# Layer 1's expert output bias: nine bf16 part pairs in one product of 96 rows instead of f32 products of 8 rows

## The chip, the cores and the metric

The kernel runs on one core of a Trainium2 chip. The core has five engines with queues of their own: TensorE (PE in the profile; its weight loads are shown apart as PEld), VectorE (DVE), ScalarE (ACT), GpSimd (POOL) and SyncE (SP), which here only issues transfers (DMAs). Each engine works through its queue in order; between engines there are semaphores. TensorE multiplies a stationary operand ("weights", loaded first) with a moving operand and writes to PSUM. The metric is the time of one execution in device microseconds (us), the median of the runs.

## The reference

Four layers act in turn on x of 625 rows (graph nodes) and 768 columns. Each layer is a graph step followed by a feed-forward step, both behind a layer norm and added to x. The feed-forward steps of layers 0, 1 and 3 are mixtures of eight experts with 192 hidden columns each; layer 1's also has attention in front, and it alone has a bias `b1` in the hidden columns and a bias `b2` of 8 x 768 at the output:

```python
        xn2 = _layernorm(x, norm2_w, norm2_b).reshape(-1, C)
        logits = xn2 @ w_gate
        top_vals, top_idx = jax.lax.top_k(logits, TOPK)
        gates = jax.nn.softmax(top_vals, axis=-1)
        gates_full = jnp.zeros((T, E), xn2.dtype).at[jnp.arange(T)[:, None], top_idx].add(gates)

        def body(acc, p):
            w1, bb1, w2, bb2, g = p
            h = jax.nn.gelu(xn2 @ w1 + bb1, approximate=False)
            return (acc + g[:, None] * (h @ w2 + bb2), None)
```

So each row of the output gets, besides the products, its eight gates times `b2`: a matrix product of 625 x 8 with 8 x 768.

## The kernel before

One program, written in program order; a scheduler orders each engine's queue by dependencies and expected times, so the queues are not always in the order of the source. The 625 rows lie in five tiles of P = 125 (`TILES`, NT = 5). All large products are in f32. One f32 product of a 128-row chunk shows in the profile as two records of L136 (in the helper `mm`) or as two matmul records of another line; a bf16 product as one.

**Experts** (`experts`, L962 and after), run for layers 0, 1 and 3:

1. `b1` and `b2` are loaded (L969 loads `b2` as `b2t`, 8 rows in f32), then the first weight matrix in three parts (L165 in `weight`; the pool of weights has four buffers, and later weights wait until an early one is free).
2. The first product makes `hg`, the 12 chunks of 128 hidden columns (8 experts x 192) for all rows, two chunks at a time, by a seven-product scheme in place of eight. `sums` (POOL, L338 to L342 in `half_products`) makes sums of weights, `first` begins a pair of chunks, `rest` ends it with PE products and DVE additions (L412) and ScalarE's gelu (L1001). `rest(c)` asks first for the sums of the next pair; the sums have two buffers, and POOL, which runs ahead, starts each when PE is through with the pair before last.
3. During the first `rest`, the router's logits (L250) are turned (L260), and `gates` (L917) computes on DVE the eight gates of each row in f32 (`lg`), and then, at L955 to L959, splits them into three bf16 parts `gb` whose sum is the f32 value: cast, subtract, cast, subtract, cast.
4. PE turns `gb` (L1025, five tiles) and DVE copies it to `gT3` (L1029): 24 rows (8 experts x 3 parts), 625 columns. In layer 1 PE also turns the f32 gates (L1033) and DVE copies them to `gT` (L1034): 8 rows.
5. `gate(c)` (L129, then L1009) spreads `gT3` with a 0/1 matrix `sel` over the chunk's 128 rows and multiplies `hg` with it, two pairs of chunks behind `rest`.
6. `down` (L1048): `hg` times the second weight matrix, quarters `q`. Tile 0 is done plainly: per half of 384 columns 12 chunks, and in layer 1 a 13th product of 8 rows, `gT` by `b2t`. Tiles 1 and 2, then 3 and 4, are done in pairs by seven products (`prod`, six chunks each); DVE makes sums of the weights (L444 to L447), POOL sums of `hg` (L464 to L468). The bias is appended to products 4, 2, 5 and 3. Product 3 enters one of the four output blocks alone, and what it adds there, together with product 5's bias of tile t + 1, has to be the bias of tile t; so it gets the difference of the gates of both tiles, `db`, made by POOL (L1094):

```python
                if b2t is not None and bias:
                    g, j = bias
                    lhs.append(db[:, t // 2] if g is None else gT[:, TILES[g]])
                    rhs.append(b2t[:, j * HD : (j + 1) * HD])
                self.mm(to, lhs, rhs)
```

The additions to x are DVE's (L1116), after a copy of the first product by ScalarE (`U`, L1124). When a tile is finished, `final` begins the next layer's norm (L178 to L191; the square root L182 is ScalarE's), and POOL adds the next layer's bias to x (L225).

**Beside layers 0 and 1's experts** runs other work of layer 3, `attention_vectors` (L1261): dot products on DVE (L1298, two for each block of weights `av_w`) with transfers of their own (L1278 `av_a`, L1287 `av_w`, two buffers). `beside(n, after)` puts n of them behind a given value (L1297 copies one element of it first).

**Around the start of layer 1's experts** SyncE's queue holds, in this order: three parts of the first weights, `b2t`, the first quarter of the second weights, `av_a` and `av_w`. On POOL stand there the sums of the first two pairs of chunks (L338 to L342), then L1525 (x plus the attention's output, last tile).

Of the kernel before, what the change touches and what calls it, by code (L numbers as in the profile page):

```python
# [9 lines left out]
F32 = mybir.dt.float32  # L10
BF16 = mybir.dt.bfloat16
# [6 lines left out]
N = 625  # L18
# [17 lines left out]
class Net:  # L36
# [880 lines left out]
    def gates(self, over_all):  # L917
# [35 lines left out]
        gb = sp.tile([P, NT, NEXP, 3], BF16, tag="gb", name="gb", bufs=1)  # L953
        r = sp.tile([P, NT, NEXP], F32, tag="gr", name="gr", bufs=1)
        nc.vector.tensor_copy(gb[:, :, :, 0], lg)  # L955
        nc.vector.tensor_tensor(r, lg, gb[:, :, :, 0], ALU.subtract)
        nc.vector.tensor_copy(gb[:, :, :, 1], r)
        nc.vector.tensor_tensor(r, r, gb[:, :, :, 1], ALU.subtract)
        nc.vector.tensor_copy(gb[:, :, :, 2], r)  # L959
        return gb  # L960

    def experts(self, over_all, w1, w2, gelu, b1=None, b2=None, after=None, beside=None):  # L962

        nc, tc, a, x = self.nc, self.tc, self.a, self.x
        with tc.tile_pool(name="moe", bufs=1) as big, ExitStack() as up_pool:
            bc = self.column(b1, NF) if b1 else None
            if b2:
                b2t = big.tile([NEXP, D], F32, name="b2t")
                nc.sync.dma_start(b2t, a[b2])  # L969
            hg = big.tile([128, NF, N], F32, name="hg")  # L970
            gT3 = big.tile([3 * NEXP, N], BF16, name="gT3")
            gT = big.tile([NEXP, N], F32, name="gT") if b2 else None
# [20 lines left out]
            def rest(c, between=None):  # L993
                if c + 2 < NF:
                    sums(c + 2)
                self.half_rest(
                    prods.pop(c), begun.pop(c), hg[:, c, :], hg[:, c + 1, :], between
                )
                for o in range(2):
                    h = self.n3(hg[:, c + o, :])  # L1000
                    nc.scalar.activation(  # L1001
                        h, h, gelu, bias=bc[:, c + o : c + o + 1] if b1 else 0.0
                    )

            def gate(c):
                gv = self.nv(self.ps(), 128)
                self.mm_nodes(gv, [sel[:, c * 128 : (c + 1) * 128]], [self.n3(gT3)])
                h = self.n3(hg[:, c, :])
                nc.vector.tensor_tensor(h, h, gv, ALU.mult)  # L1009
# [6 lines left out]
            turned, gb = self.logits(big), []  # L1016

            def choose():
                turned()
                gb.append(self.gates(over_all))  # L1020

            rest(0, choose)
            pv = self.nv(self.ps(), 3 * NEXP)
            for t in range(NT):
                nc.tensor.matmul(  # L1025
                    pv[:, t, :], gb[0][:, t].rearrange("p e i -> p (e i)"), self.identb[:P, :P],
                    start=True, stop=True,
                )
            nc.vector.tensor_copy(self.n3(gT3), pv)  # L1029
            if b2:  # L1030
                pv = self.nv(self.ps(), NEXP)
                for t in range(NT):
                    nc.tensor.transpose(pv[:, t, :], self.lg[:, t, :], self.ident[:P, :P])  # L1033
                nc.vector.tensor_copy(self.n3(gT), pv)  # L1034
            for c in range(2, NF + 2, 2):
                if c < NF:
                    if c not in begun:
                        first(c)
                    rest(c)
                for o in (c - 2, c - 1):  # L1040
                    gate(o)
                if beside and c < NF:
                    beside(1, hg[:P, c + 1, 0:1])
            up_pool.close()
            with tc.tile_pool(name="moedown", bufs=1) as dp:
                self.down(dp, a[w2], hg, gT, b2t if b2 else None, after, beside)

    def down(self, pool, w2, hg, gT, b2t, after, beside):  # L1048
# [14 lines left out]
        if b2t is not None:  # L1063
            db = pool.tile([NEXP, 2, P], F32, name="db")
# [7 lines left out]
        for j in range(2):  # L1072
            lhs = [hg[:, c, TILES[0]] for c in range(NF)]
            rhs = [q[c // HB][j][:, c % HB, :] for c in range(NF)]
            if b2t is not None:
                lhs.append(gT[:, TILES[0]])
                rhs.append(b2t[:, j * HD : (j + 1) * HD])
            self.mm(p[:, 512 * j : 512 * j + HD], lhs, rhs)
# [12 lines left out]
        def sums(t):  # L1091
            if b2t is not None:

                nc.gpsimd.tensor_tensor(  # L1094
                    db[:, t // 2], gT[:, TILES[t]], gT[:, TILES[t + 1]], ALU.subtract
                )
            prods[t] = list(zip(self.left_sums(pool, hg, t), rights))

        sums(1)
        for t in (1, 3):  # L1100
# [4 lines left out]
            def prod(n, to, bias=None):  # L1105
                A, B = pr[n - 1]
                lhs = [A[:, c, :] for c in range(HB)]
                rhs = [B[:, c, :] for c in range(HB)]
                if b2t is not None and bias:
                    g, j = bias  # L1110
                    lhs.append(db[:, t // 2] if g is None else gT[:, TILES[g]])
                    rhs.append(b2t[:, j * HD : (j + 1) * HD])
                self.mm(to, lhs, rhs)
# [17 lines left out]
            prod(4, b2, (t + 1, 0))  # L1131
# [10 lines left out]
            prod(2, a1, (t, 0))  # L1142
# [4 lines left out]
            prod(5, a2, (t + 1, 1))  # L1147
# [4 lines left out]
            prod(3, b1, (None, 1))  # L1152
# [1150 lines left out]
```

## Time and profile before

| what | value |
|---|---|
| three runs, median (lowest to highest) | 1932.52 us (1931.92 to 1932.81) |
| the profiled execution, its own time | 1933.47 us |
| its span, first to last instruction | 1931.8 us |
| PE busy, share of the span | 1855.9 us, 96% |
| DVE, ACT, POOL busy | 59%, 27%, 31% |
| mean granted clock of TensorE | 0.986 of full |
| DMA, mean | 53 GB/s |
| layer 0's, 1's and 3's turn of the gates (L1025) starts at | 258.97, 750.14, 1800.62 us |
| products with `b2t` in layer 1: records, first and last start | 20, from 816.2 to 892.2 us |

"Busy" counts the time in which an engine has an instruction in flight. TensorE's matmuls overlap each other and their ends are modelled, so the time between two starts says more than a record's length. "<-" behind a wait names what released it. A "stretch" is a piece of the span between two times.

### The profile page before, as it was taken

What the parts mean: (1) busy time and instruction counts of PE and PEld (TensorE: products, weight loads), DVE (VectorE), ACT (ScalarE), POOL (GpSimd) and SP (SyncE); (2) the same over time, 40 slices, a digit from 0 to 9 for tenths busy, and PEclk for the clock granted to TensorE, in tenths of its full rate; (3) what the DMA queues carried; (4) which work ended last, traced back from release to release, by engine and by line L of the source; (5) the groups of instructions that cost most, each with busy time, mean ns of one, the idle gap of its engine ahead of it and who ended that gap; (6) DMA issues with size and microseconds to landing.
All of it is one profiled execution on the core that took longest, in us unless ns stands there. A gap on an engine that the chain in (4) does not pass through costs nothing.

```text
span 1931.8 us, 21712 instructions
## 1 busy us (share of the span) xinstructions
PE 1855.9 (96%) x8314; PEld 1274.8 (66%) x8314; DVE 1134.9 (59%) x2226; ACT 526.2 (27%) x961; POOL 601.8 (31%) x515
## 2 busy tenths in 40 slices
PE   7968899999999999999999999999999999999999
PEld 6844565555677766655556778878667888556665
DVE  8789857647566756674835464554546555145562
ACT  2379611002254532100111131322314233111200
POOL 1079624234410052343015222231035321402331
PEclk9969899999999999999999999999999999999999
DMA  2040112120300022213510211000011121020111
GB/s 68 21 142 37 36 37 66 53 80 12 103 26 25 1 96 90 71 52 115 156 65 31 76 36 63 26 25 33 1 43 35 39 71 65 1 98 25 47 35 32
DMA packets 64021, 103.16 MB, mean 53 GB/s; under 512 B 7301, under 2 KB 37223, under 8 KB 63918
## 3 DMA queue, kind: packets, MB, share of 16 engines
q1 hardware_dynamic: 63658, 101.69, 16.2%
q8 instruction: 66, 1.08, 0.2%
q14 instruction: 37, 0.30, 0.1%
q10 hardware_dynamic: 260, 0.09, 0.0%
HBM read 99.81 MB, written 1.95 MB: 53 GB/s over the span
## 4 chain that ended last, share of the span: by engine, by line
PE 83%; DVE 7%; POOL 4%; ACT 2%; issue 1%; DMA 1%; SPq 1%; ACTq 0%; DVEq 0%; POOLq 0%
PE ps L136 65%; PE ps L129 3%; POOL gat_w L560 2%; PE ps L777 2%; PE ps L1806 2%; PE ps L1461 2%; PE ps L1493 2%; PE ps L1480 1%; PE ps L198 1%; PE ps L1675 1%; PE ps L143 1%; DMA av_w<-in_L_gnn_W 1%; PE ps L715 1%; DVE gat_w L591 1%; ACT gat_w L593 1%
## 5 line engine op out<-in xcount | busy, mean ns | idle before, releaser
L338 POOL TENSOR_TENSOR S<-w 128x384 f32<-128x384 f32 x40 | 41.5, 1042 | 453.6 <-PE ps L136 354.8
L136 PE MATMUL ps<-xT,w 128*128 128x313 f32 x480 | 137.9, 431 | 0.7 <-ACT pr L1469 0.7
L136 PE MATMUL ps<-w,xT 128*125 128x384 f32 (+2 forms) x392 | 125.3, 473 | 0.0
L136 PE MATMUL ps<-T,w 128*128 128x313 f32 x408 | 121.5, 428 | 0.0
L560 POOL TENSOR_TENSOR gat_w<-gat_w,xT 125x625 f32<-125x625 f32 x60 | 86.3, 1469 | 101.0 <-DVE xT L532 94.0
L136 PEld LDWEIGHTS ps<-xT,w 128*128 128x128 f32 x480 | 89.1, 190 | 35.1 <-issue 2.7
L136 PE MATMUL ps<-T,S 128*128 128x313 f32 x348 | 107.5, 444 | 1.8 <-DVE T L318 1.4
L136 PEld LDWEIGHTS ps<-w,xT 128*125 128x125 f32 x392 | 72.8, 188 | 46.6 <-issue 11.7
L136 PE MATMUL ps<-w,S 128*125 128x384 f32 x292 | 100.2, 488 | 2.8 <-DVE x L1116 2.8
L136 PE MATMUL ps<-xT,S 128*128 128x313 f32 x336 | 102.7, 433 | 0.0
L136 PE MATMUL ps<-w,hg 128*125 128x384 f32 x288 | 96.5, 488 | 0.9 <-DVE hg L1009 0.9
L136 PEld LDWEIGHTS ps<-T,w 128*128 128x128 f32 x408 | 76.0, 189 | 29.9 <-DVE U L358 1.4
L136 PE MATMUL ps<-hh,gat_w 125*125 125x257 f32 (+1 forms) x400 | 89.8, 379 | 0.0
L136 PEld LDWEIGHTS ps<-T,S 128*128 128x128 f32 x348 | 65.6, 195 | 30.7 <-issue 5.1
L136 PE MATMUL ps<-w,x2T 128*125 128x384 f32 (+1 forms) x280 | 84.1, 449 | 0.0
L136 PEld LDWEIGHTS ps<-w,S 128*125 128x125 f32 x292 | 54.3, 188 | 43.9 <-DVE x L1116 4.0
L136 PEld LDWEIGHTS ps<-hh,gat_w 125*125 125x125 f32 x400 | 73.3, 187 | 11.3 <-issue 0.4
L136 PEld LDWEIGHTS ps<-w,hg 128*125 128x125 f32 x288 | 53.1, 188 | 39.9 <-issue 2.2
L777 PE MATMUL ps<-ohd,ohs 125*125 125x313 bf16 x425 | 66.4, 312 | 12.2 <-DVE ohs L770 12.2
L136 PEld LDWEIGHTS ps<-xT,S 128*128 128x128 f32 x336 | 61.0, 189 | 25.0 <-issue 4.1
L1298 DVE CUSTOM_DVE_ANT_0 av_junk<-av_w,av_a 128x512 f32<-128x512 f32 (+1 forms) x80 | 72.2, 902 | 8.9 <-DMA av_w<-in_L_gnn_W 7.2
L569 DVE CUSTOM_DVE_ANT_0 junk<-ps,mb 125x625 f32<-125x625 f32 x85 | 68.5, 806 | 13.5 <-PE ps L143 8.7
(442 smaller groups left out, 3795.9 us busy)
## 6 DMA issues: line engine op xcount, KB each, us to landing
w<-in_L_ffn_phiT SPq DMA_DIRECT2D x8, 1536.0 KB
w<-in_L_gnn_W SPq DMA_DIRECT2D x8, 1536.0 KB
w<-in_L_ffn_w SPq DMA_DIRECT2D x6, 1152.0 KB
w<-in_L_gnn_W SPq DMA_DIRECT2D x6, 1152.0 KB
av_w<-in_L_gnn_W SPq DMA_DIRECT2D x24, 256.0 KB
av_w<-in_L_gnn_W SPq DMA_DIRECT2D x16, 384.0 KB
w<-in_L_ffn_w SPq DMA_DIRECT2D x3, 1536.0 KB
w<-in_L_ffn_qkv_wT SPq DMA_DIRECT2D x6, 768.0 KB
```

The source lines that it names most:

```text
L129: self.nc.tensor.matmul(pv[:, s, :], lhs[i], rhs[i][:, s, :], start=i == 0, stop=i == n - 1)
L136: self.nc.tensor.matmul(out, lhs[i], rhs[i], start=i == 0, stop=i == n - 1)
L143: self.nc.tensor.transpose(pv[:, t, :], col(t).to_broadcast([P, rows]), self.ident[:P, :P])
L198: nc.tensor.transpose(pv[:, k, :P], src[:, k * 128 : (k + 1) * 128], self.ident[:P, :P])
L338: nc.gpsimd.tensor_tensor(S1, A21, A22, ALU.add)
L560: nc.gpsimd.tensor_tensor(w[:, s, :], w[:, s, :], lc[:, s, :], ALU.add)
L569: nc.vector.tensor_tensor_reduce(self.n3(junk), row, self.n3(mb[:, t, :]), 1.0, -3e38, ALU.subtract, ALU.max, m[:, t : t + 1],)
L777: nc.tensor.matmul(acc[j // 2][:, j % 2, :], ohs[:, TILES[j]], ohd[:, 0:HN], start=c == cs[0], stop=c == cs[-1],)
L1298: nc.vector.tensor_tensor_reduce(junk, wt, row, 1.0, 0.0, ALU.mult, ALU.add, dst)
L1461: nc.tensor.matmul(sv[r][:, s, :], qk[half[r], 0, TILES[t]], self.n3(qk[half[r], 1, :])[:, s, :], start=True, stop=True,)
L1493: nc.tensor.matmul(ov[half[r]], v[:, s, h * DH : (h + 1) * DH], pT[r][:, s, :], start=s == 0, stop=s == NT - 1,)
L1806: nc.tensor.matmul(pv[:, j, :], zTs[t][:, k, :], w2[k // 3][:, k % 3, js], start=k == 0, stop=False,)
```

## The change

- `gates` no longer makes a tile of its own, but writes into a tile `gb` that `experts` makes: for each row of x, `copies` groups of `rows` columns. In layers 0 and 3 this is one group of 24, as before; in layer 1 three groups of 32 (24 used, the rest set to zero by POOL). The third part is written directly by the last subtraction, in all three layers. In layer 1 two copies bring the 24 columns to the other groups.
- `gT3` has 96 rows in layer 1: three groups of the 24 parts of the gates. The f32 turn and `gT` are gone; `gate` reads the first 24 rows.
- `b2` is loaded nine times, so that 96 rows hold it: row 32 j + 3 e + i is `b2` of expert e (i and j from 0 to 2); the rows between are zero (POOL). `bias_parts`, seven operations of POOL behind the `rest` of chunks 6 and 7, makes the bf16 tile `b2p`: in group j the j-th bf16 part of `b2`. One product of 96 rows thus sums all nine pairs of a gate part and a bias part. `b2n` is the right half of it with the sign changed.
- In `down` the bias products are `gT3` by `b2p`, in bf16. Product 3 has two of them, tile t by the right half of `b2p` and tile t + 1 by `b2n`, in place of one by `db`; POOL's `db` is gone.

```diff
         nc.vector.tensor_tensor(lg, lg, den.to_broadcast([P, NT, NEXP]), ALU.mult)
-        gb = sp.tile([P, NT, NEXP, 3], BF16, tag="gb", name="gb", bufs=1)
         r = sp.tile([P, NT, NEXP], F32, tag="gr", name="gr", bufs=1)
-        nc.vector.tensor_copy(gb[:, :, :, 0], lg)
-        nc.vector.tensor_tensor(r, lg, gb[:, :, :, 0], ALU.subtract)
-        nc.vector.tensor_copy(gb[:, :, :, 1], r)
-        nc.vector.tensor_tensor(r, r, gb[:, :, :, 1], ALU.subtract)
-        nc.vector.tensor_copy(gb[:, :, :, 2], r)
-        return gb
+        parts = gb[:, :, 0, 0 : 3 * NEXP].rearrange("p t (e i) -> p t e i", i=3)
+        nc.vector.tensor_copy(parts[:, :, :, 0], lg)
+        nc.vector.tensor_tensor(r, lg, parts[:, :, :, 0], ALU.subtract)
+        nc.vector.tensor_copy(parts[:, :, :, 1], r)
+        nc.vector.tensor_tensor(parts[:, :, :, 2], r, parts[:, :, :, 1], ALU.subtract)
+        for j in range(1, gb.shape[2]):
+            nc.vector.tensor_copy(gb[:, :, j, 0 : 3 * NEXP], gb[:, :, 0, 0 : 3 * NEXP])
...
+            copies, rows = (3, 32) if b2 else (1, 3 * NEXP)
             if b2:
-                b2t = big.tile([NEXP, D], F32, name="b2t")
-                nc.sync.dma_start(b2t, a[b2])
+
+                b2t = big.tile([96, D], F32, name="b2t")
+                b2p = big.tile([96, D], BF16, name="b2p")
+                b2n = big.tile([96, D // 2], BF16, name="b2n")
+                nc.gpsimd.memset(b2t, 0.0)
+                for j in range(3):
+                    for i in range(3):
+                        r = 32 * j + i
+                        nc.sync.dma_start(b2t[r : r + 3 * NEXP - 2 : 3, :], a[b2])
             hg = big.tile([128, NF, N], F32, name="hg")
-            gT3 = big.tile([3 * NEXP, N], BF16, name="gT3")
-            gT = big.tile([NEXP, N], F32, name="gT") if b2 else None
+            gT3 = big.tile([copies * rows, N], BF16, name="gT3")
+            gb = big.tile([P, NT, copies, rows], BF16, name="gb")
+            if b2:
+                nc.gpsimd.memset(gb, 0.0)
...
+            def bias_parts(after):
+
+                nc.gpsimd.tensor_copy(b2p[:, 0:1], after)
+                nc.gpsimd.tensor_copy(b2p, b2t)
+                nc.gpsimd.tensor_tensor(b2t, b2t, b2p, ALU.subtract)
+                for j in range(1, 3):
+                    nc.gpsimd.tensor_copy(b2p[32 * j : 32 * j + 32, :], b2t[32 * j : 32 * j + 32, :])
+                nc.gpsimd.tensor_tensor(b2p[64:96, :], b2t[64:96, :], b2p[64:96, :], ALU.subtract)
+                nc.gpsimd.tensor_scalar(b2n, b2p[:, D // 2 :], -1.0, None, ALU.mult)
...
-            pv = self.nv(self.ps(), 3 * NEXP)
+            pv = self.nv(self.ps(), copies * rows)
...
             nc.vector.tensor_copy(self.n3(gT3), pv)
-            if b2:
-                pv = self.nv(self.ps(), NEXP)
-                for t in range(NT):
-                    nc.tensor.transpose(pv[:, t, :], self.lg[:, t, :], self.ident[:P, :P])
-                nc.vector.tensor_copy(self.n3(gT), pv)
...
                     rest(c)
+                    if b2 and c == 6:
+                        bias_parts(hg[:96, 5, 0:1])
...
-            if b2t is not None:
+            if bias:
                 lhs.append(gT[:, TILES[0]])
-                rhs.append(b2t[:, j * HD : (j + 1) * HD])
+                rhs.append(bias[0][:, j * HD : (j + 1) * HD])
...
-            if b2t is not None:
-
-                nc.gpsimd.tensor_tensor(
-                    db[:, t // 2], gT[:, TILES[t]], gT[:, TILES[t + 1]], ALU.subtract
-                )
...
+            bl, br, bn = bias[0][:, 0:HD], bias[0][:, HD:], bias[1]
...
-            prod(4, b2, (t + 1, 0))
+            prod(4, b2, (t + 1, bl))
...
-            prod(2, a1, (t, 0))
+            prod(2, a1, (t, bl))
...
-            prod(5, a2, (t + 1, 1))
+            prod(5, a2, (t + 1, br))
...
-            prod(3, b1, (None, 1))
+            prod(3, b1, (t, br), (t + 1, bn))
```

In the order of instructions of the changed kernel, which is fixed before it runs, nothing moves on ScalarE. On SyncE the first quarter of the second weights now stands ahead of the loads of `b2`. On DVE, in layer 1's first pair of tiles, the addition of product 2 to x (L1116) stands one dot product (L1298) earlier than before, and the additions of products 5 and 3 keep their place or stand up to one dot product earlier.

## The prediction

> **What bounds the kernel now.** I read first the share of the chain that ended last, by engine; then the list of what TensorE waits for; then the timeline of the three places where layer 1's bias and the gates are made; then the table of busy time by stretch with the granted clock; last, the comparison of the two kernels' instruction order, which needs no run.
>
> ```profile
> PE 83%; DVE 7%; POOL 4%; ACT 2%; issue 1%; DMA 1%; SPq 1%; ACTq 0%; DVEq 0%; POOLq 0%
> ```
> TensorE (PE) carries 83% of the chain: an instruction taken from PE is time, except where PE soon waits for something else. Those waits, in the list of waits of PE (total us, times, longest):
> ```profile
> PE ps L1025 <- DVE gb L959: 7.8, 3, 2.6
> ...
> PE ps L136 <- DVE x L1116: 2.8, 2, 1.6
> ```
> The change touches both. The first is the turn of the gates, once in each expert layer (0, 1, 3): PE has nothing to do for 2.6 us until VectorE (DVE) has split the gates in three bf16 parts. Layer 0, timeline (start, us, engine, line):
> ```profile
> 256.92 0.99 POOL L341 TENSOR_TENSOR w<-w 128x384 f32<-128x384 f32 x1
> 257.05 0.92 DVE L958 TENSOR_TENSOR gr<-gr,gb 125x40 f32<-125x40 f32 x1
> 257.87 0.99 POOL L342 TENSOR_TENSOR S<-w,S 128x384 f32<-128x384 f32 x1
> 258.00 0.92 DVE L959 CAST gb<-gr 125x40 bf16<-125x40 f32 x1
> 258.82 0.47 DVE L412 TENSOR_TENSOR hg<-hg,ps 128x313 f32<-128x313 f32 x1
> 258.97 0.27 PEld L1025 LDWEIGHTS <-gb 125*24 125x24 bf16 x5 [3.11 <-DVE gb L959]
> 258.97 0.45 PE L1025 MATMUL ps<-identb,gb 125*24 125x125 bf16 x5 [2.61 <-DVE gb L959]
> ```
> A DVE operation on 40 elements should be short: the cast of L955, before GpSimd (POOL) starts, takes 0.21. Those at L956 to L959 take 0.6 to 1.0, and each ends just after a POOL operation of L338 to L342 ends. While POOL works, each such step costs one POOL operation, whatever its size. And the wait has an after-effect (stretch; span of it and busy us of PE, PEld, DVE, ACT, POOL with counts; PEclk is the granted clock):
> ```profile
> 256.10:259.51 3.41, 0.80 (x7) 0.43 (x7) 3.17 (x5) 0.19 (x1) 2.76 (x3) 1.00 0.00 0
> 259.51:262.93 3.42, 3.42 (x7) 2.23 (x8) 0.92 (x2) 0.53 (x1) 0.00 (x0) 0.50 0.00 0
> 747.62:751.03 3.41, 0.89 (x10) 0.70 (x11) 3.17 (x5) 0.54 (x1) 2.41 (x3) 1.00 0.00 0
> 751.03:754.45 3.42, 3.42 (x9) 2.31 (x8) 1.12 (x3) 0.27 (x1) 0.00 (x0) 0.50 0.00 0
> ...
> 1798.92:1802.34 3.42, 1.72 (x10) 1.32 (x11) 2.78 (x4) 0.72 (x1) 1.59 (x2) 1.00 0.02 5
> 1802.34:1805.75 3.41, 3.41 (x14) 2.28 (x13) 0.71 (x2) 0.00 (x0) 0.00 (x0) 1.00 0.00 0
> ```
> A stretch of 3.41 us with PE busy 0.80 or 0.89 (23%, 26%) is followed by one at half clock, in layers 0 and 1. In layer 3 the same wait straddles two stretches, the emptier one is 50% busy, and the clock stays.
>
> **The change, part by part.** The sum is made against the profiled execution, 1933.47 us (span 1931.8 and 1.7 around it); the median of the runs, 1932.52, is 0.95 lower.
>
> (a) *Gates of layers 0 and 3.* One of the four DVE steps in POOL's shadow goes: the last subtraction writes bf16 itself. L958 ended at 257.97, L959 at 258.92: 0.95 us earlier for PE, twice: 1.9. From there the chain is PE, and the weight loads and POOL sums behind it are released by PE, so the gain travels on.
>
> (b) *The clock in layer 0.* With a wait of 2.61 - 0.95 = 1.66 us no stretch of 3.41 can be less than 51% busy, wherever it begins; 50% kept the clock in layer 3. So 259.51 to 262.93 should run at full clock: 3.42 / 2 = 1.7. Bounds 0 and 1.7; I take 1.7. [...]
>
> (c) *Gates of layer 1.* Here DVE has one step more: five become six (two copies of 24 bf16 columns added, one cast gone). The four POOL operations there end at 750.02 and L959 at 750.09; the first copy takes its place, the second follows when POOL is done: 0.2, the duration of L955 (0.95 if it had to wait for POOL again). Five f32 transposes of the gates (L1033, 750.51 to 751.05) go: -0.54. The turn now has 96 columns of weights, not 24: 0 to 0.13, as a 128-column load (L198) takes 0.13 and five follow each other. Sum -0.2, bounds -0.35 and +0.55. The wait stays near 2.7 us, so I leave layer 1's half clock where it is. L1034's copy (0.79 on DVE) goes too, before a DVE wait of 2.3 on PE: nothing.
>
> (d) *The price of a bias product.* PE rows, of layer 1's first output tile and of a gate product (24 rows, bf16) between f32 products:
> ```profile
> 816.22 0.91 PE L136 MATMUL ps<-b2t,gT 8*125 8x384 f32 x2
> ...
> 817.05 7.39 PEld L136 LDWEIGHTS ps<-w,hg 128*125 128x125 f32 x24 [0.55 <-issue]
> ```
> ```profile
> 756.96 0.69 PE L136 MATMUL ps<-T,S 128*128 128x313 f32 x2
> ...
> 757.58 0.38 PE L129 MATMUL ps<-gT,sel 24*128 24x500 bf16 x1
> ...
> 757.89 0.53 PE L136 MATMUL ps<-xT,S 128*128 128x313 f32 x1
> ```
> Starts count, since ends are modelled. Two records of 384 columns in a stream are 0.322 apart (six in 1.93 at 707.85 to 709.78). Old product: 816.22 to 817.05 is 0.83; the records before it (four from 814.83) are 0.10 late, and so is the second record behind it: 1.03 in all. bf16: two f32 records of 0.263 from 756.96 leave 0.09 to 757.58, then 0.31 to 757.89, and again 0.10 behind (0.53 against 0.43 long): 0.51 for 500 columns. Three gate products (125, 500, 125) at 761.26 take 0.42 to the next f32: 250 columns more for 0.11, 0.44 ns a column. So 384 columns cost 0.51 - 0.05 = 0.46, and a second product behind it 0.17. Saved: 0.57 where one replaces one, 0.40 at the two places where two replace one. No row has 96 rows of weights between products of 128; bounds: 0.17 alone (saves 0.86) and the old 1.03 for each (saves nothing); I take the gate product, the same type between the same neighbours.
>
> (e) *Where it arrives.* Tile 0 has two of them, 1.14; but the product after next waits for ScalarE's copy of U (L1124), which stands behind L182 (828.99, 0.29), which hangs on DVE's sums L444 to L447 and not on PE. Copy from 829.28, 0.48 long: that product starts at 829.8 in place of 830.60, so 0.8 arrives. Then DVE is the chain:
> ```profile
> 847.72 0.69 DVE L1298 CUSTOM_DVE_ANT_0 av_junk<-av_w,av_a 128x512 f32<-128x512 f32 x1
> ...
> 850.08 0.69 DVE L1298 CUSTOM_DVE_ANT_0 av_junk<-av_w,av_a 128x512 f32<-128x512 f32 x1 [1.66 <-DMA av_w<-in_L_gnn_W]
> ...
> 850.70 0.55 DVE L1116 TENSOR_TENSOR x<-x,ps 125x384 f32<-125x384 f32 x1
> ...
> 851.30 4.13 PE L136 MATMUL ps<-w,S 128*125 128x384 f32 x12 [1.61 <-DVE x L1116]
> ```
> PE's product waits for the addition at 850.70, which stands behind a dot product that waits for a transfer. The bias products at 843.05 and 847.30 lie before this wait and alone bring nothing. But in the order of the changed kernel that addition stands ahead of this dot product: it can start at 848.42, 2.28 earlier. PE is then released at 851.30 - 0.8 - 2.3 = 848.2 (its own work would let it start at 847.5). From there PE is the chain: 0.57 + 0.40 in this pair of tiles, 3 x 0.57 + 0.40 in the next: 3.1. Together 6.2. If the next pair's copy of U is held by L182 again (it has 0.3 us of room), up to 0.7 is lost.
>
> (f) *What is added off the path.* POOL: two memsets between L342 (ends 725.35) and L1525 (starts 726.90): 0.8 (0.52 for 128x512) and 0.4 to 0.5 (1.37 for 1536 bf16), in an idle time of 1.55. On SyncE nine loads of b2 in place of one, each some 0.43 to issue, the eighth behind the landing of the w2 quarter issued at 725.67; av_a behind them moves from 731.67 to about 732.3, and the first dot product is at 763.97. The preparation of b2's parts: seven POOL operations behind the sums that end at 775.36. By L225 (1.8 for 768) for two, memset (1.0 ns an element) to L225 for the copies: 6.5 to 10.2 us, ending at 782 to 786. The next sums begin at 782.66, take 4.9, and are needed at 798.41: 7.9 us of cover remain at the worst. The DVE product of gate 5 now waits for POOL's first small copy (775.5), at 783.
>
> Sum: 1.9 + 1.7 + 0.2 + 6.2 = 10.0. From 1933.47 that is 1923.5, from the median 1922.5; I forecast 1923.
>
> **The rivals.** 1. *The order of DVE brings nothing*: the dot products slip, or the addition meets its own wait; 2.3 stay: 1925.3. For it: DVE is late there because of transfers; against: three dot products before it have their data by 847. 2. *The clock stays as it is*: 259.5 to 262.9 runs at half clock anyway, or the runs without a profile had it full already: 1924.7. For it: the median lies 0.95 under the profiled run, so in other runs layer 0's wait may have straddled two stretches and cost no half clock; against: the six rows above. [...] 3. *Little arrives*: the 96-row product costs what the old one did, the second one on top, and 1. and 2. hold: 1.9 + 0.8 of gain less 0.6: some 1930.5. 4. *Slower: the parts of b2 make POOL late.* POOL has 798.4 - 775.4 - 4.9 = 18.1 us for them; beyond that the last sums hold PE, and at 18.1 + 10 = 28 us the gain is gone. L274's copies speak for it (1.01 us for 48 elements, 21 ns each; at that price three copies are 48 us: 1923 + 40 = 1963); against: L274 ran beside a DVE operation of 0.94 that ended with it, and here DVE reads PSUM for most of the time.
>
> **How the numbers follow.** Forecast 0.52, rival 1 0.18, rival 2 0.15, rival 3 0.08, rival 4 0.07. No change means within 0.2%, 3.9 us (about what a measurement of this kernel can tell): above 1928.65. Faster 0.52 + 0.18 + 0.15 = 0.85, same 0.08, slower 0.07. The range goes down by layer 1's half clock (1.7) and cheaper products (0.3 on six of them): 1919.5; up to rivals 1 and 2 together with (c) at its worst: 1923 + 2.3 + 1.7 + 0.6 = 1927.6. That leaves out some 2 in 10.
>
> **What would show it.** In layers 0 and 3 PE waits about 1.65 for the gates; no half clock behind layer 0's. Bias products as single bf16 records, next f32 start about 0.25 to 0.3 later. The addition after 847 with no transfer ahead of it, and PE's wait for L1116's line gone or under 0.8. POOL done with b2's parts before 787. The forecast is wrong if PE waits for the last half sums of the experts' first product, or if the bias product stays above 0.8.

## The result, and the profile after

| | before | after |
|---|---|---|
| median of the runs, us | 1932.66 (1931.92 to 1933.35, 4 runs) | 1918.44 (1916.16 to 1920.57, 4 runs) |
| ratio, 95% interval | | 0.9928 [0.9915, 0.9942] |
| profiled execution (span), us | 1933.47 (1931.8) | 1920.57 (1918.8) |
| TensorE waits for the gates, layers 0, 1, 3, us | 2.61, 2.59, 2.61 | 1.67, 2.67, 1.68 |
| first bias product to the next f32 record (starts), us | 0.83 | 0.17 |

The kernel is 14.2 us faster; the forecast was 10 less, and its range ended 1.1 us above the median. In a later comparison the same two kernels stood at 1933.4 and 1919.94 us (9 and 5 runs), ratio 0.993 [0.9918, 0.9943].

The profile after, first the chain that ended last, by engine, then four rows of the list of what PE waits for (total us, times, longest):

```profile
PE 83%; DVE 9%; ACT 3%; POOL 2%; DMA 1%; issue 1%; ACTq 0%; DVEq 0%; POOLq 0%; SPq 0%
...
PE ps L136 <- ACT U L1139: 3.4, 4, 1.2
PE ps L1047 <- DVE gb L958: 3.4, 2, 1.7
...
PE ps L1047 <- DVE gb L960: 2.7, 1, 2.7
...
PE ps L136 <- DVE x L1131: 2.1, 2, 1.1
```
The waits for the gates of layers 0 and 3 went from 2.6 to 1.7 us each; layer 1's, now behind the second copy of the parts (L960), stayed at 2.7; the wait for the addition to x fell from at most 1.6 to 1.1. New in size is the wait for ScalarE's copy of U (L1139): bias products that cost less reach it sooner.

Layer 0's gates, timeline of the kernel after (start, us, engine, line):

```profile
254.44 0.99 POOL L339 TENSOR_TENSOR S<-S,w 128x384 f32<-128x384 f32 x1
254.46 1.04 DVE L957 CAST gb<-gr 125x40 bf16<-125x40 f32 x1
255.40 0.99 POOL L341 TENSOR_TENSOR w<-w 128x384 f32<-128x384 f32 x1
255.53 0.94 DVE L958 TENSOR_TENSOR gb<-gr,gb 125x40 bf16<-125x40 f32 x1
256.35 1.01 POOL L342 TENSOR_TENSOR S<-w,S 128x384 f32<-128x384 f32 x1
...
256.52 0.45 PE L1047 MATMUL ps<-identb,gb 125*24 125x125 bf16 x5 [1.67 <-DVE gb L958]
```
The last step writes bf16 itself, so PE is released one POOL operation earlier. The granted clock in the stretches of 3.41 us around layer 0's and layer 1's wait (columns as before: stretch; span, busy us of PE, PEld, DVE, ACT, POOL; PEclk is the 1.00 or 0.50 near the end):

```profile
254.33:257.74 3.41, 1.74 (x10) 0.97 (x10) 3.17 (x5) 0.94 (x2) 2.95 (x4) 1.00 0.00 0
257.74:261.15 3.41, 3.41 (x14) 2.45 (x13) 0.55 (x2) 0.00 (x0) 0.00 (x0) 1.00 0.00 0
742.43:745.85 3.42, 0.96 (x4) 0.38 (x2) 3.32 (x7) 0.82 (x1) 3.34 (x4) 1.00 0.00 0
745.85:749.26 3.41, 3.19 (x10) 2.34 (x11) 1.26 (x3) 0.82 (x1) 0.02 (x1) 0.50 0.00 0
```
Layer 0 keeps its clock (PE busy 1.74 of 3.41, 51%); layer 1 (0.96, 28%) is halved as before. Then the first bias product:

```profile
810.38 1.13 PE L136 MATMUL ps<-w,hg 128*125 128x384 f32 x3
...
811.03 0.14 PEld L136 LDWEIGHTS <-gT 96*125 96x125 bf16 x1
811.35 0.33 PE L136 MATMUL ps<-b2p,gT 96*125 96x384 bf16 x1
...
811.52 1.13 PE L136 MATMUL ps<-w,hg 128*125 128x384 f32 x3
```
Its weights are loaded at 811.03, one record ahead; it starts on time, 0.32 after the record before it, and the next starts 0.17 later. ("Late" is here and below what a start lies behind the even distance of the stream, 0.32.) Nothing is late on either side: 0.17 in all, where the old product cost 1.03. Last, DVE's order in the first pair of tiles:

```profile
842.65 0.55 DVE L1131 TENSOR_TENSOR x<-x,ps 125x384 f32<-125x384 f32 x1
...
843.25 2.52 PE L136 MATMUL ps<-w,S 128*125 128x384 f32 x7 [0.93 <-DVE x L1131]
844.89 0.69 DVE L1314 CUSTOM_DVE_ANT_0 av_junk<-av_w,av_a 128x512 f32<-128x512 f32 x1 [1.11 <-DMA av_w<-in_L_gnn_W]
```
The addition stands ahead of the dot product that waits for its transfer until 844.89. PE goes on at 843.25, 8.05 us earlier than before, though it still waits 0.93 for this addition.

Where the time went, from the starts of the same PE records in both first profiles: 1.5 us before the gates of layer 0, where nothing was changed; 0.95 and 1.68 in layer 0's gates (wait, clock); 0.64 in layer 1's; 7.08 in layer 1's down product; 1.08 from there to layer 3's turn. 12.9 in all.

### The profile page after: what moved, and what is told of

Its sections match the earlier page's. It is cut to its first block, busy times and chain, and to the rows that moved or that the text cites. A ratio compares the mean times of both kernels' runs of the same rounds, so it can differ in the third digit from the quotient of the medians.

```text
span 1918.8 us, 21705 instructions
## 1 busy us (share of the span) xinstructions
PE 1847.8 (96%) x8301; PEld 1272.9 (66%) x8301; DVE 1131.2 (59%) x2224; ACT 526.1 (27%) x961; POOL 609.9 (32%) x522
## 3 DMA queue, kind: packets, MB, share of 16 engines
q8 instruction: 66, 1.08, 0.2%
## 4 chain that ended last, share of the span: by engine, by line
PE 83%; DVE 9%; ACT 3%; POOL 2%; DMA 1%; issue 1%; ACTq 0%; DVEq 0%; POOLq 0%; SPq 0%
PE ps L136 63%; PE ps L129 4%; PE ps L777 3%; PE ps L1822 2%; PE ps L1477 2%; PE ps L1509 2%; PE ps L1496 1%; POOL gat_w L560 1%; PE ps L198 1%; ACT gat_w L593 1%; PE ps L143 1%; PE ps L1691 1%; DMA av_w<-in_L_gnn_W 1%; DVE gat_w L591 1%; DVE av_junk L1314 1%
## 5 line engine op out<-in xcount | busy, mean ns | idle before, releaser
L136 PEld LDWEIGHTS ps<-hh,gat_w 125*125 125x125 f32 x400 | 73.3, 187 | 11.3 <-issue 0.4
L129 PE MATMUL ps<-gat_w,ft 125*65 125x500 f32 (+1 forms) x240 | 74.9, 470 | 4.4 <-DVE gat_w L591 3.1
L777 PE MATMUL ps<-ohd,ohs 125*125 125x313 bf16 x425 | 65.5, 309 | 12.2 <-DVE ohs L770 12.2
```

The costliest lines, as they stand in the source:

```text
L129: self.nc.tensor.matmul(pv[:, s, :], lhs[i], rhs[i][:, s, :], start=i == 0, stop=i == n - 1)
L136: self.nc.tensor.matmul(out, lhs[i], rhs[i], start=i == 0, stop=i == n - 1)
L777: nc.tensor.matmul(acc[j // 2][:, j % 2, :], ohs[:, TILES[j]], ohd[:, 0:HN], start=c == cs[0], stop=c == cs[-1],)
```

## The experiments

**1. How many rows make a bias product cheap?** The changed kernel with the first 32, 64 or 65 rows of both operands of the bias product; the bf16 parts of b2 in the other rows are left out of the sum.

```diff
-                self.down(dp, a[w2], hg, gT3, (b2p, b2n) if b2 else None, after, beside)
+                self.down(
+                    dp, a[w2], hg, gT3[0:32] if b2 else gT3,
+                    (b2p[0:32], b2n[0:32]) if b2 else None, after, beside,
+                )
```
32 rows:

> The changed kernel, but its bias products use only the first 32 of the 96 rows (group 0: the three gate parts by the first bf16 part of b2), so the second and third parts of b2 are left out of the output; all queues keep their order. Question: why a bias product cost PE 0.17 us (start 811.351 to the next f32 start 811.518, weights loaded ahead) and not the 0.46 that the gate product of 24 rows suggested. Theory A, the number of rows: weights in one group of 32 rows are not loaded ahead next to weights of 128 rows, those in three groups are; then each product shows a gap before its weight load and costs 0.45 to 0.5. Theory B, something else of the gate product (its 128 columns of output, its place behind a chunk of 313 columns): the product stays at 0.17. Only the distance of starts is read.

64 rows:

> As rows32, with the first 64 rows (gate parts by the first two bf16 parts of b2; the third is left out). Theory A with a border between one group of 32 rows and more: 0.17 as with 96. Theory A with a border at half of the array: 0.45 to 0.5. Theory B: 0.17.

65 rows:

> The changed kernel with its bias products over the first 65 of the 96 rows (rows 64 and 65 to 95, the last parts, are left out or zero in the sum). With 64 rows the product cost 0.50 as with 32, with 96 rows 0.17. Theory J (what counts is more than 64 rows): the next f32 product starts 0.17 us after the bias product and nothing is late before it, the whole down product as in the changed kernel. Rival K (the 96 rows themselves, or all four quarters of the rows, or a smooth growth): 65 rows cost 0.50 as 64 do, the time is that of 64 rows, 0.3 us a product longer.

Measured, one run each: 1923.81, 1920.56 and 1921.81 us. The times alone mislead, since the part before layer 0's gates varies (experiment 6); the rows of the timelines tell. 32 rows:

```profile
812.60 0.81 PE L136 MATMUL ps<-w,hg 128*125 128x384 f32 x2
813.34 0.13 PEld L136 LDWEIGHTS <-gT 32*125 32x125 bf16 x1 [0.55 <-issue]
813.34 0.37 PE L136 MATMUL ps<-b2p,gT 32*125 32x384 bf16 x1
813.64 0.29 PEld L136 LDWEIGHTS ps<-w,hg 128*125 128x125 f32 x2 [0.17 <-issue]
```
65 rows:

```profile
811.74 0.81 PE L136 MATMUL ps<-w,hg 128*125 128x384 f32 x2
812.07 0.14 PEld L136 LDWEIGHTS <-gT 65*125 65x125 bf16 x1
812.39 0.33 PE L136 MATMUL ps<-b2p,gT 65*125 65x384 bf16 x1
...
812.55 0.49 PE L136 MATMUL ps<-w,hg 128*125 128x384 f32 x1
```
With 32 rows the load of the weights starts with the product itself (both 813.34), 0.09 late, the next f32 record follows 0.30 later and the one behind it is again 0.10 late: 0.50. With 64 rows the starts are the same to 0.01 us. With 65 rows the load is one record ahead (812.07) and the product costs 0.17, as with 96. So the step lies between 64 and 65 rows (theory J), and 0.17 is not a gift of the 96 rows. Why the load waits with 64 rows (0.50) and not with 65 (0.17) no run here shows.

Layer 1's down product is 6.11 and 6.07 us shorter than before in the 32- and 64-row kernels, 7.24 with 65 rows. The forecast, with its price of 0.46, had 6.2 there.

**2. The f32 product, padded to 96 rows.** The kernel before, its operands filled with zero rows:

```diff
-                b2t = big.tile([NEXP, D], F32, name="b2t")
-                nc.sync.dma_start(b2t, a[b2])
+                b2t = big.tile([96, D], F32, name="b2t")
+                nc.gpsimd.memset(b2t, 0.0)
+                nc.sync.dma_start(b2t[0:NEXP], a[b2])
...
-            gT = big.tile([NEXP, N], F32, name="gT") if b2 else None
+            gT = big.tile([96, N], F32, name="gT") if b2 else None
```


> The kernel before with its f32 bias products widened from 8 to 96 rows by zeros (POOL sets them, the f32 products stay, DVE's order stays the old one, gates as before). Theory A (rows): the two records lose their gaps and a product costs 0.645 in place of 1.03; tile 0 gains 0.77, the products 4 and 2 of the first pair nothing since the addition behind the waiting dot product stays where it was, the six products behind it 0.39 each: 0.77 + 2.3 = 3.1 us faster than the kernel before, near 1929.5. Theory B (the two f32 records themselves are the price): no change, 1932.6.

Measured: 1931.49 us against 1933.93 (10 and 14 runs), ratio 0.9986 [0.9976, 0.9996]: a small gain, as theory A had it (2.4 for the 3.1 expected). The two records now take 0.65 with nothing late, 0.38 less a product than 1.03. This kernel has the old order of DVE, and its timeline shows what that costs:

```profile
848.92 0.69 DVE L1301 CUSTOM_DVE_ANT_0 av_junk<-av_w,av_a 128x512 f32<-128x512 f32 x1 [1.65 <-DMA av_w<-in_L_gnn_W]
...
849.53 0.55 DVE L1119 TENSOR_TENSOR x<-x,ps 125x384 f32<-125x384 f32 x1
...
850.14 0.91 PE L136 MATMUL ps<-w,S 128*125 128x384 f32 x2 [2.40 <-DVE x L1119]
```
The addition stands behind the dot product and its transfer, PE's wait grows from 1.61 to 2.40, and PE's records, 1.85 us ahead of the kernel before until here (0.43 of it from ahead of the down product), are 1.16 ahead behind it. Without the new order of DVE the cheap products gave back 0.69 of these 1.85 us at this place.

**3. The shorter split alone.** The kernel before, with the last subtraction writing the bf16 part:

```diff
-        nc.vector.tensor_tensor(r, r, gb[:, :, :, 1], ALU.subtract)
-        nc.vector.tensor_copy(gb[:, :, :, 2], r)
+        nc.vector.tensor_tensor(gb[:, :, :, 2], r, gb[:, :, :, 1], ALU.subtract)
```


> The kernel before with one edit: the last subtraction of the gates writes the third bf16 part itself, in all three layers; nothing else of the change. Theory C (each step costs one POOL operation, and a wait of 1.66 us keeps the clock): 0.95 three times, and 1.7 for each half clock that goes, layers 0 and 1: 2.9 + 3.4 = 6.3 us in the profile, 1.2 us or more less in the median where other runs had the clock: 1926 to 1928. [...]

Measured: 1927.47 us (1927.11 to 1929.17, 5 runs) against 1933.93, ratio 0.9966 [0.9953, 0.9979]. All three waits are 1.66 to 1.68, and none is followed by a half clock: 0.95 in each of three layers, and 1.6 to 1.7 of clock in layers 0 and 1. One line is worth 6 us, 2.6 of it in layer 1, where the full change put two copies in the place of the step it saved.

**4. Do DVE's small steps wait for POOL?** The changed kernel, with POOL's third group of half sums held by a one-column copy that needs the finished parts:

```diff
+        if after is not None:
+            nc.gpsimd.tensor_copy(S1[:P, 0, 0:1], after)
...
-                ))
+                ), after=gb[:, 0, copies - 1, 2:3] if c == 4 else None)
```


> The changed kernel with GpSimd's third group of half sums held back, by a one-column copy that needs the last bf16 part of the gates, until VectorE has split the gates. Nothing else moves. Theory E (each short VectorE step on SBUF waits out one GpSimd operation, whatever its size): the steps of the split take 0.2 us each in place of 0.7 to 1.04; TensorE's wait for the gates, 1.67 in layers 0 and 3, goes to nothing, and layer 1's 2.4 goes with its half clock (1.7): up to 7.4 us less than the changed kernel, unless GpSimd's sums, which start some 0.9 us later than without the hold, then release the weight loads behind them late. Rival F (the steps are slow by themselves, or wait for the tables of the gates): the steps keep their 0.9 us and GpSimd is only later: no gain, or up to 3 us slower.

Measured: 1914.22 us (1913.5 to 1914.72, 4 runs) where the changed kernel beside it had 1919.94: 5.7 less. Timeline, layer 0:

```profile
254.08 0.19 DVE L958 TENSOR_TENSOR gr<-lg,gb 125x40 f32<-125x40 f32 x1
...
254.31 0.21 DVE L959 CAST gb<-gr 125x40 bf16<-125x40 f32 x1
254.55 0.23 DVE L960 TENSOR_TENSOR gb<-gr,gb 125x40 bf16<-125x40 f32 x1
254.91 0.19 POOL L339 CAST S<-gb 125x1 f32<-125x1 bf16 x1 [15.89 <-DVE gb L960]
...
255.16 0.45 PE L1049 MATMUL ps<-identb,gb 125*24 125x125 bf16 x5
```
The same steps take 0.2 in place of 0.7 to 1.0, and PE doesn't wait (0.2 in layer 1). POOL's sums, later now, hold nobody. From the wait to the end its profile is 7.5 us shorter than the changed kernel's with a half clock in layer 1, 5.0 than without. So the steps are slow beside POOL, and not by themselves (theory E, against rival F). Why they take 0.7 to 1.0 beside POOL and 0.2 without it no run here shows.

**5. More rows for the gate products too.** `sel` and `gT3` get 96 rows, 24 to 95 zero, in all three layers:

```diff
-        self.sel = self.const.tile([3 * NEXP, NEXP, FF], BF16, name="sel")
+        self.sel = self.const.tile([96, NEXP, FF], BF16, name="sel")
...
-            copies, rows = (3, 32) if b2 else (1, 3 * NEXP)
+            copies, rows = (3, 32) if b2 else (1, 96)
...
-            if b2:
-                nc.gpsimd.memset(gb, 0.0)
+            nc.gpsimd.memset(gb, 0.0)
...
-                self.mm_nodes(gv, [sel[:, c * 128 : (c + 1) * 128]], [self.n3(gT3[0 : 3 * NEXP, :])])
+                self.mm_nodes(gv, [sel[:, c * 128 : (c + 1) * 128]], [self.n3(gT3)])
```


> The changed kernel with the gate products of all three layers taken over 96 rows in place of 24 (rows 24 to 95 are zero in both operands, so the sums are the same). Theory A (weights of 64 rows or fewer aren't loaded ahead beside f32 products of 128 rows, weights of 96 rows are): each entry into gate products costs 0.30 us less, as between the bias product of 32 rows (0.50) and that of 96 (0.17 to 0.20); there are some ten entries a layer in three layers, so about 9 us, less 0.25 us in layers 0 and 3 for the turn of the gates with 96 columns in place of 24: 8 to 9 us less than the changed kernel, if TensorE is what sets the end there. Rival B (the bf16 parts of b2 were cheap for another reason than their rows): gate products stay at 0.51, and the kernel is 0.5 us slower.

The control of these runs, the changed kernel itself:

> The changed kernel itself, as the control of this batch, on the chip of the experiments. If the result is that of the change and not of the chip, it stands 13 to 16 us below the kernel before (ratio 0.992 to 0.993), as on the first chip. Its profile shows whether the half clock in layer 1 behind the turn of the gates (745.8 to 749.3 in the first profile) and the three half clocks of layer 0's graph step (151.9, 169.0 and 186.1) come again at the same places. Theory G (the phase of the clock's 3.41 us stretches against the work decides, and it is new in every run): the ones in the graph step come and go from run to run and account for a spread of 2 to 4 us; layer 1's is there in most runs, since a wait of about 2.4 us empties a stretch in most phases. Rival H: places and number are the same in every run.

Measured: 1913.44 us (1912.18 to 1914.7, 4 runs), 6.5 less than the control's 1919.94 (1918.71 to 1921.62, 5 runs). The same group of three gate products in the control:

```profile
265.90 0.69 PE L136 MATMUL ps<-xT,S 128*128 128x313 f32 x2
...
266.52 0.49 PE L129 MATMUL ps<-gT,sel 24*128 24x125 bf16 x3
...
266.94 0.53 PE L136 MATMUL ps<-T,S 128*128 128x313 f32 x1
```
and with 96 rows:

```profile
271.33 0.69 PE L136 MATMUL ps<-xT,S 128*128 128x313 f32 x2
...
271.86 0.49 PE L129 MATMUL ps<-gT,sel 96*128 96x125 bf16 x3
...
272.19 0.48 PE L136 MATMUL ps<-xT,w 128*128 128x313 f32 x1
```
From the first of the two f32 records to the f32 record behind the group it is 1.04 against 0.86, and 0.05 more is saved behind it: 0.24 a group (0.62 to 0.38, the lateness on both sides counted in), not the 0.30 expected. A single gate product saves 0.14 and the last seven of a layer lose 0.09. With five singles and four groups of three a layer that would be 1.6; the part of each layer with gate products is in fact 1.30, 1.34 and 1.64 shorter, 4.3 in all, since in layers 0 and 1 PE, earlier now, waits once for an addition of DVE (0.28 and 0.29).

The other 2 us have another cause: PE's wait for the gates is 0.7 here in layers 0 and 3, not 1.7, since the cast of L957 took 0.22 in place of 1.04. That is no chance. The tile `gb` has rows of 24 columns in the kernel before and in layers 0 and 3 of the changed kernel, and of 96 in its layer 1 and in all layers here. Beside POOL's L339, which starts 0.01 to 0.02 us ahead of it, L957 took 1.03 or 1.04 in all 36 places where the row has 24 columns, and 0.22 or 0.23 in all 12 where it has 96 (all profiles but the two with POOL held back). So not every short step of DVE waits for POOL: this cast waits only with the narrow row. Why the row decides no run here shows. The expected 8 to 9 came from a price too high for most groups, in part made up by a gain it had not seen.

Both edits in one:

> Both edits in one. If theories E and A hold and the two gains lie at different places (the turn of the gates, the products behind it), they add: up to 16 us less than the changed kernel, about 1903, which is below both kernels. If the weight loads or GpSimd become the bound behind the turn of the gates, the sum is smaller than the two parts; then waits of TensorE for half sums stand in layer 0 behind 258 us.

Measured: 1909.80 us (1908.17 to 1910.2, 4 runs) against 1933.4 for the kernel before, ratio 0.9877 [0.9863, 0.989]: the best of all, 10.1 less than the changed kernel. The expected 16 was too much; the two gains as measured, 5.7 and 6.5, would make 12.2, and the 2 us of the wait for the gates in layers 0 and 3 stand in both. What the wide gate products bring on top of the hold is 4.4 by the medians, and 3.6 behind the wait in the two profiles below.

**6. What differs between runs of one kernel?** The medians lie 13.5 to 14.2 apart, the first two profiles 12.9, of which 1.5 lie where nothing was changed. More profiles of both kernels, unchanged:

> The kernel before, one more profile of it, to see where the clock is halved. Theory G (the phase of the 3.41 us stretches against the work decides): the 2.6 us waits for the gates in layers 0, 1 and 3 are each followed by a half clock in most profiles but not in all, not in the same ones (so far: layer 0 and 1 in the first profile, all three in that with 96 zero-padded f32 rows, none of layer 3 in the first). If a stretch is halved when it was less than half busy, the wait must lie in one stretch with 1.7 us or more; that is so in 77% of the phases. Rival H: the same places as in the first profile, layers 0 and 1, never layer 3.

> As the run before it: a third profile of the kernel before. Theory G: some of layers 0, 1 and 3, about three in four, and other places in the graph step than in the first profile. Rival H: layers 0 and 1 again, and the graph step as in the first.

> A third profile of the changed kernel. Theory G: never a half clock behind the 1.67 us waits of layers 0 and 3; behind layer 1's 2.7 us in most profiles (two of two so far); the graph step's ones at one to four places. Rival H: the same places as in the first profile of it.

> A further profile of the changed kernel. Its three profiled runs so far took 1920.6 to 1921.6, and its runs without a profile mostly 1916.2 to 1920.3 at a higher granted clock. Theory L (half clocks before 258 us come and go; the work behind that is alike in every run): if this run is below 1920, the half clocks missing in it are those before 258 us, and from the turn of the gates in layer 0 to the end it takes the same 1661 to 1663 us as in the other profiles. Rival M (fast runs have no half clock behind layer 1's turn of the gates, or a wait less in layer 1's down product): then the part behind 258 us is 1.5 us or more shorter.

> As the run before it: one more profile of the changed kernel, the same two theories with the same numbers.

> As the two runs before it: one more profile of the changed kernel, the same two theories with the same numbers.

> A fourth profile of the kernel before. Theory L: from the turn of the gates in layer 0 to the end it takes 1671.5 to 1673 us as in its three profiles so far, with half clocks in layers 0 and 1 and none in layer 3; any other difference in time lies before 258 us. Rival M: half clock behind layer 3's wait too, 1.7 longer.

Here each profile is cut where PE begins to wait for the gates of layer 0, ahead of everything the change touches (turn's start less its wait, from the timelines; us; the time is 1.7 more than the two parts together):

| kernel, profile | time | up to the wait | wait to the end | half clock behind the waits of layers 0, 1, 3 |
|---|---|---|---|---|
| before, first | 1933.47 | 256.4 | 1675.4 | yes, yes, no |
| before, a and b | 1932.64, 1932.29 | 255.7, 255.4 | 1675.2, 1675.2 | yes, yes, no |
| before, c | 1930.39 | 253.2 | 1675.5 | yes, no, yes |
| f32 padded | 1932.25 | 255.9 | 1674.6 | yes, yes, yes |
| split alone | 1927.11 | 255.9 | 1669.5 | no, no, no |
| 32, 64 rows | 1923.81, 1920.56 | 256.5, 253.5 | 1665.6, 1665.4 | no, yes, no |
| 65 rows | 1921.81 | 255.8 | 1664.3 | no, yes, no |
| after, first | 1920.57 | 254.9 | 1664.0 | no, yes, no |
| after, again and c | 1921.62, 1921.29 | 255.8, 254.7 | 1664.1, 1664.9 | no, yes, no |
| after, f | 1922.06 | 256.1 | 1664.2 | no, yes, no |
| after, d and e | 1916.67, 1918.66 | 253.6, 255.2 | 1661.4, 1661.8 | no, no, no |
| hold | 1913.50 | 255.2 | 1656.6 | no, no, no |
| gates 96 | 1912.18 | 253.5 | 1657.0 | no, no, no |
| both | 1908.17 | 253.5 | 1653.0 | no, no, no |

Up to the wait it is 253.2 to 256.5 us, in every kernel, with no order among them: this part varies from run to run, as theory L had it. Behind it the kernel before took 1675.2 to 1675.5 in all four profiles (in c one half clock has only changed its layer); the changed kernel has two values, 1664.0 to 1664.9 and 1661.4 to 1661.8 (d, e and f were taken in one batch on one chip). That is theory M, for profiles d and e. Timeline of profile f, layer 1, the cast of L957 and the two copies that fill the parts of the gates out to 96 rows (merged in one row):

```profile
744.25 0.99 POOL L339 TENSOR_TENSOR S<-S,w 128x384 f32<-128x384 f32 x1
744.27 0.23 DVE L957 CAST gb<-gr 125x40 bf16<-125x40 f32 x1
...
745.21 0.99 POOL L341 TENSOR_TENSOR w<-w 128x384 f32<-128x384 f32 x1
745.36 1.84 DVE L960 COPY gb<-gb 125x120 bf16<-125x120 bf16 x2
746.16 0.99 POOL L342 TENSOR_TENSOR S<-w,S 128x384 f32<-128x384 f32 x1
```
and of profile d:

```profile
742.79 0.98 DVE L960 COPY gb<-gb 125x120 bf16<-125x120 bf16 x2
743.58 1.05 POOL L342 TENSOR_TENSOR S<-w,S 128x384 f32<-128x384 f32 x1
...
743.92 0.45 PE L1047 MATMUL ps<-identb,gb 125*96 125x125 bf16 x5 [1.82 <-DVE gb L960]
```
The first copy takes 0.89 in both. In d the second gets through beside L342 and takes 0.17; in f it waits for all of it, 1.03. PE's wait is 1.8 against 2.7, and with it goes the half clock: 0.9 + 1.6 = 2.5. Each time the copy and L342 start within 0.02 us of each other, so the start times don't tell which wins.

Windows of d and of the kernel before, c, show behind which stretches the clock is halved. d, layer 1:

```profile
741.42:744.84 3.42, 1.60 (x11) 0.99 (x10) 3.07 (x7) 1.29 (x2) 3.13 (x4) 1.00 0.00 0
744.84:748.25 3.41, 3.41 (x15) 2.44 (x14) 0.85 (x2) 0.17 (x1) 0.00 (x0) 1.00 0.01 2
```
Before, c, layers 0, 1 and 3:

```profile
253.78:257.20 3.42, 1.44 (x9) 1.11 (x10) 3.03 (x5) 0.73 (x1) 1.87 (x2) 1.00 0.00 0
257.20:260.61 3.41, 3.41 (x8) 2.13 (x8) 0.48 (x1) 0.00 (x0) 0.00 (x0) 0.50 0.00 0
745.30:748.72 3.42, 1.77 (x14) 1.37 (x15) 3.22 (x5) 0.82 (x1) 1.54 (x2) 1.00 0.00 0
748.72:752.13 3.41, 3.41 (x15) 2.44 (x14) 0.70 (x2) 0.00 (x0) 0.00 (x0) 1.00 0.01 2
1793.19:1796.61 3.42, 0.81 (x8) 0.59 (x8) 3.18 (x5) 0.42 (x1) 2.54 (x3) 1.00 0.00 0
1796.61:1800.02 3.41, 3.41 (x8) 2.30 (x7) 1.00 (x2) 0.31 (x1) 0.00 (x0) 0.50 0.00 0
```
In c, layer 1's wait of 2.6 us straddles two stretches (PE 52% busy in the one shown) and the clock stays; layer 3's lies in one (24%) and the clock is halved. So the places are not fixed to a layer (against rival H), though three of four profiles of the kernel before agree. Around the waits for the gates, each stretch in which PE was 22 to 30% busy was followed by a half clock, and so was one of 42% (c, layer 0); those of 47% (d and e) and more were not. The expectation's "less than half busy" was a little too wide.

## Why the forecast was right in direction and too small

Two steps failed. Step (d) priced a bias product at 0.46 us where it cost 0.17. Step (c) took 0.2 for the second copy (0.95 as its bound), saw no shorter step in the split, and left layer 1's half clock where it was; the copy takes 1.03 or 0.17, a cast ahead of it 0.22 in place of 1.04, and where both are short the half clock goes. Point by point:

(a) *Gates of layers 0 and 3*: right, 0.95 each. Its reading that each short step beside POOL costs one POOL operation holds for these layers (0.6 to 1.04 us a step), but not for L957 in layer 1 (0.22).

(b) *The clock in layer 0*: right, 1.68 for 1.7. No stretch behind a wait of 1.7 us (1.66 to 1.68) was halved in any of the profiles.

(c) *Gates of layer 1*: wrong, though the wait came out as forecast in four profiles, 2.67 for "near 2.7". That was luck: two errors cancel. The forecast let the first copy end where L959 had ended, behind L342, and the second follow 0.2 later. In fact the first copy ends one POOL operation earlier, with L341, since L957 takes 0.22 in layer 1 and not 1.04 (experiment 5); and the second copy then waits for L342, 1.03. The turn saved 0.64, more than its bound of 0.35: the transposes 0.54; against it the wider turn 0.15 (0.13 at most in the forecast, from a load of L198, which takes 0.14) and the wait 0.08; the rest because the half clock now begins 0.2 before PE has work. In profiles d and e the second copy takes 0.17, near its price; then the wait is 1.8 and the half clock goes, some 2.5 more.

(d) *The price of a bias product*: the term that was mis-sized. Forecast 0.46 and 0.17 for a second, measured 0.17 and 0.33 for both together. It was taken from the gate product as the nearest row in type and neighbours; what decided is that this one has 24 rows of weights, and the bias product 96 (experiment 1: 0.50 with 32 and 64 rows, 0.17 with 65). The lower bound, 0.17, was the answer. With 32 rows the forecast's price is nearly met (0.50), and that kernel is 9.8 us shorter behind the wait (1675.4 to 1665.6), where the forecast had 10.0 in all.

(e) *Where it arrives*: right in every place, but for one sign. Tile 0 kept 0.9 of 1.63, since the copy of U holds the product after next (0.8 forecast); products 4 and 2 and the new order of DVE brought 2.38 (2.3); the later six brought 4.60, at 0.70 to 0.86 each, of which the second pair's copy of U took back 0.80 ("up to 0.7"): 3.8 (3.1). Sum 7.08 for 6.2. Of the 0.3 us by which each product was cheaper than forecast, less than half reached the end: experiment 1's 6.11 with 32 rows against 7.08. PE's wait for the addition was to be gone or under 0.8; it is 0.93, since PE comes there sooner (with 32 rows it is 0.33). The 847.5 for PE's own work should have been 847.75 by the terms beside it (851.30 less 1.61, 0.8 and twice 0.57); nothing rests on it.

(f) *Off the path*: right. b2's parts took POOL from 770.55 to 778.06, 7.5 us (6.5 to 10.2), and the next sums start behind them at 778.04, 0.15 later than PE would have released them (782.66 less the 4.77 gained until then); PE waits for none of them. Of the rivals, 1, 3 and 4 fell; 2 fell for layer 0.

So: 10.0, with 0.9 for (d) and 0.4 for (c) makes 11.3; measured behind the wait 10.3 to 11.5 with layer 1's half clock (11.4 in the first profiles), 13.4 to 14.1 without it. The forecast's range had allowed for that half clock and for cheaper products, but not for the 0.9 of wait that goes with it.

The medians are 13.5 to 14.2 apart; in the first comparison the changed kernel's, 1918.44, lies 4.6 under the forecast of 1923. By the table a run with layer 1's half clock takes 1918.9 or more (253.2 + 1664.0 + 1.7), and a run without it 1920.0 or less (256.5 + 1661.8 + 1.7). The seven runs of the changed kernel without a profile took 1916.16, 1917.68, 1918.71, 1918.88, 1919.2, 1919.94 and 1920.26. The first three would thus be runs without the half clock, two of them in the first comparison, the last one a run with it, and the others could be either. That would make the half clock of step (c) the largest part of the miss. No trace shows these runs, so this is argued and not shown.

## What to carry to other kernels

A small bf16 product between f32 products of 128 rows was cheap here only where its weights had more than 64 rows (the bias product 0.17 us with 65 and 96, 0.50 with 32 and 64): padded with zeros to 96, a group of three gate products of this kernel cost 0.38 in place of 0.62, and all of them together 4.3 us less. Short DVE steps on the critical path took 0.7 to 1.0 us beside POOL, but for the cast with the wide row, and 0.2 without it: holding POOL's next group back until they were through was worth 5.7 us for one added copy of a column in each layer. A wait of PE was worth more than its length where it emptied a stretch of 3.41 us: from 2.6 to 1.7 us, 0.9 brought 2.6 (experiment 3, layer 1).

## What was not expected of the hardware

That the loading ahead of these weights has a step between 64 and 65 rows (0.50 against 0.17 us a product). That the cast L957 of DVE on 40 elements waited for a POOL operation that started 0.01 to 0.02 us ahead of it when it wrote rows of 24 columns (1.04), and did not when it wrote into rows of 96 (0.22). That a copy of 0.17 and a POOL operation which started within 0.02 us of each other went either way (0.17 in profile d, 1.03 in f), so that one kernel has two times, some 2.5 us apart. And that the nine loads of b2, with 8 rows of every third partition each, took SyncE 0.62 to 0.74 us each to issue, where the one load of 8 neighbouring rows had taken 0.29, though nothing waited for them.
